# A two-layer graph network on one core: attention scores on four tiles of the array, and the softmax sums on two

## The chip, the core and the metric

The kernel runs on one core of a Trainium2 chip. The metric is the device time of one execution in microseconds (us), lower is better. All data is float32.

## The reference

`x` has 16 graphs of 1024 nodes with 256 channels. Layer 0 normalizes each node, builds a weighted adjacency from the difference of the nodes' channel means, makes queries from it, keys and values from the normalized nodes, and runs attention with four heads of 64 channels. Layer 1 normalizes again, multiplies by a normalized adjacency, and applies two linear maps with a batch norm each. Both layers add their result to `x`. The change lies in the attention of layer 0:

```python
q = jnp.transpose(g, (0, 2, 1)).reshape(B, N, h, hd).transpose(0, 2, 1, 3)
kv = (x @ kv_w).reshape(B, N, 2, h, hd).transpose(2, 0, 3, 1, 4)
k, v = (kv[0], kv[1])
scale = (1.0 + 1e-06) / (np.sqrt(hd) + 1e-06)
attn = jax.nn.softmax(jnp.einsum('bhnd,bhmd->bhnm', q, k) * scale, axis=-1)
out = jnp.einsum('bhnm,bhmd->bhnd', attn, v)
```

## The kernel before, in words

The 16 graphs go through `attention()` (L1032) in 64 **units**: a graph `b`, a pair of heads `k` (two heads of 64 channels fill the 128 partitions), and a half `f` of the 1024 queries (FB = 512). A unit has four **steps**; a step `g` takes two blocks `m` of 128 keys. So there are 256 steps. Each step issues on TensorE, in this order:

- `scores` (L906): for each of the two key blocks, one tile `sc` of two PSUM banks; for each head `e` of the pair a matmul (L914) whose weights are 64 channels by 128 keys and whose moving operand is 64 channels by 512 queries. Head 0 lies in rows 0 to 63 of the array, head 1 in rows 64 to 127. ScalarE then takes the exponential of the 128x1024 tile into `p` (L922).
- What `at_top` holds for this step: the `sums` (L977) of the unit before, or its `finish` (L1004), four transposes of 128x128.
- `values` (L946) of the step before: for each key block and head a matmul (L955) whose weights are 128 keys by 64 channels, so that head 0 fills array columns 0 to 63 and head 1 columns 64 to 127; they accumulate in `o` over the four steps of a unit.
- Pieces of the **background** (L818): everything else of the neighbouring graphs (queries, keys and values, layer 1's aggregation and first linear map). It is a chain of Python generators; each piece names a cost, and the loop at L1077 draws pieces until the cost done has reached the cost due at this step. Nearly all matmuls of the background go through `product` (L168), which splits a 128x128 weight block into two column halves of 64 (`HW`), each a matmul with all 128 rows.

The softmax isn't shifted by its maximum. The denominators come from VectorE: `add` (L935) sums the `p` tiles of a unit into `acc`; at the end of two steps `fold` (L966) transposes squares of `acc` and sums them into `part`. Three steps after the unit's last values, `sums` multiplies `part` (32 columns) by the constant matrix `same` in one matmul of 128x128 weights (L985), and three VectorE instructions (L993 to L1002) pick and invert the sums. One step later `finish` transposes the output and `add_output` scales it and adds it to `x`.

The order on every engine is the order of the Python calls (`manual_schedule`, L1421). Inside a step it is: scores, `at_top`, a piece of the background that asked for the top of a step (`TOP`, only in graph 0, two pieces with transposes), `adds`, `add`, `values`, background, `at_end`. For the last unit (`UNITS - 1`) sums and finish are one step after its last values, both in `at_top`.

After the loop comes `second` (L1143): the second linear map of layer 1 in matmuls of 128x128 weights (L1259), transposes back (L1390) and the output's DMAs. A second, shifted path (`shifted_attention`, L861) runs only if the sums leave a safe range; it isn't run here.

Of the kernel before, what the change touches and what calls it, by code (L numbers as in the profile page):

```python
# [17 lines left out]
P = 128  # L18
# [5 lines left out]
def gnn_two_layers_kernel(  # L24
# [12 lines left out]
    nc = tc.nc  # L37
# [6 lines left out]
    FB = 512  # L44
# [3 lines left out]
    HW = P // 2  # L48
# [27 lines left out]
    UNITS = B * CC * NH  # L76
# [20 lines left out]
    def layers(shifted):  # L97
# [23 lines left out]
        xs, hs, hts, ats, qs, ks, vs = {}, {}, {}, {}, {}, {}, {}  # L121
# [11 lines left out]
        def advance(pieces):  # L133

            due = queue[:]
            queue.clear()
            cost = next(pieces, None)
            for action in due:
                action()
            return cost  # L140

        def run(*parts):
            for part in parts:
                while advance(part) is not None:
                    pass
            while queue:
                queue.pop(0)()
# [20 lines left out]
        def product(dst, left, right, start, stop):  # L168

            for e in range(2):  # L170
                r = slice(e * HW, (e + 1) * HW)
                nc.tensor.matmul(dst[r], left[:, r], right, start=start, stop=stop)  # L172
# [645 lines left out]
        def background(b):  # L818

            if b == 0:  # L820
                differences(1)
                for k in range(CC):
                    yield TOP
                    transposed(1, k)
                    yield 1.0
                w, products, norm = weighers[1], keys_values(1), Norm(2, True).all()
                yield from weave(
                    islice(products, 4), (0, double(islice(w, 8))), (0, islice(norm, 4))
                )
                yield from weave(  # L830
                    plain_queries(1), (0, norm), (0, w), (5, graph()), (7, degrees())
                )
                differences(2)
                yield from islice(products, 2)
                yield from prepare(2, products)
                return
            before = hidden(b - 1)
            gather = aggregate(b - 1)
            if b + 1 < B:
                w, products, norm = weighers[b + 1], keys_values(b + 1), normed(b - 1)  # L840
                yield from weave(islice(products, 4), (0, islice(w, 4)))
                if b == 1:
                    load_later()
                yield from weave(queries(b + 1), (0, double(w)), (9, islice(norm, 5)))
                yield next(gather)
                yield from weave(products, (0, norm))
            else:
                yield from weave(endings.pop(), (2, normed(b - 1)))
                yield next(gather)
            if b + 2 < B:  # L850
                yield from weave(gather, (3, summed(b + 2)))
                yield from prepare(b + 2, before)
            elif b + 2 == B:

                yield from gather
                endings.append(before)
            else:
                yield from gather
                yield from weave(before, (0, normed_last()))
# [46 lines left out]
        def scores(b, k, f, g):  # L906


            made = []
            for m in (2 * g, 2 * g + 1):  # L910
                sc = ps_sc.tile([P, 2, FB], F32, tag="sc", name=f"sc_{b}_{k}_{f}_{m}")
                for e in range(2):
                    r = slice(e * HD, (e + 1) * HD)
                    nc.tensor.matmul(  # L914
                        sc[:, e, :],
                        ks[b][k][r, m * P : (m + 1) * P],
                        qs[b][k][r, f * FB : (f + 1) * FB],
                        start=True,
                        stop=True,
                    )  # L920
                pr = p4.tile([P, 2, FB], F32, tag="p", name=f"p_{b}_{k}_{f}_{m}")
                nc.scalar.activation(pr, sc, AF.Exp)  # L922
                made.append(pr)
            return made

        class Unit:
# [50 lines left out]
            def sums(self):  # L977

                b, k, f = self.at
                J = FB // P  # L980
                if k == f == 0:
                    invs[b] = p2.tile([P, CC, NH, J, 2], F32, tag="inv", name=f"inv_{b}")
                self.inv = invs[b][:, k, f]
                pt = ps_t.tile([P, FB], F32, tag="t", name=f"sums_{self.name}")[:, : 2 * J * NS]
                nc.tensor.matmul(  # L985
                    pt,
                    same.rearrange("p a r -> p (a r)"),
                    self.part.rearrange("p e c -> p (e c)"),
                    start=True,
                    stop=True,  # L990
                )
                tmp = p1.tile([P, 2 * J, NS + 1], F32, tag="group", name=f"group_{self.name}")
                nc.vector.tensor_mul(  # L993
                    tmp[:, :, :NS],
                    pt.rearrange("p (c a) -> p c a", a=NS),
                    group.unsqueeze(1).to_broadcast([P, 2 * J, NS]),
                )
                nc.vector.tensor_reduce(tmp[:, :, NS], tmp[:, :, :NS], AX.X, ALU.add)
                nc.vector.reciprocal(
                    self.inv.rearrange("p j e -> p e j"),  # L1000
                    tmp[:, :, NS].rearrange("p (e j) -> p e j", e=2),
                )  # L1002
# [29 lines left out]
        def attention():  # L1032

            units = [Unit(b, k, f) for b in range(B) for k in range(CC) for f in range(NH)]
            steps = [(u, g) for u in units for g in range(NG)]
            per_graph = CC * NH * NG
            before = None
            at_top, at_end, adds = {}, {}, {}
            bg, done, total, top = iter(()), 0.0, 0.0, False
            for s in range(len(steps) + 2):  # L1040
                if s < len(steps):
                    unit, g = steps[s]
                    b = unit.at[0]
                    if s % per_graph == 0:
                        run(bg)
                        top = False
                        bg, done = background(b), 0.0
                        total = (37.6 if b > 0 else 41.0) * (b + 1 < B) + 24.0 * (b > 0) + 4.0 * (b + 2 < B)
                        total += 13.7 * (0 < b < B - 2) + 27.4 * (b == B - 1) + 3.0 * (b == 0)

                        total -= 10.3 * (b == B - 1)
                    made = scores(*unit.at, g)
                    due = total * (s % per_graph + 1) / per_graph
                else:
                    due += 5.1
                for action in at_top.pop(s, ()):
                    action()
                if top:
                    done += advance(bg)
                    top = False  # L1060
                if s in adds:
                    adds.pop(s)()
                if s < len(steps):
                    for pr in made:
                        unit.add(pr)
                if before is not None:
                    (last, g_last), prs = before
                    last.values(g_last, prs)
                    if g_last == NG - 1:

                        one = (0, 0, 1, 1) if last.index == UNITS - 1 else (0, 1, 3, 4)
                        for e in range(2):
                            at_end.setdefault(s + one[e], []).append(lambda u=last, e=e: u.fold(e))
                        at_top.setdefault(s + one[2], []).append(last.sums)
                        at_top.setdefault(s + one[3], []).append(last.finish)
                        adds[s + one[3]] = last.add_output
                while done < due and not top:  # L1077
                    cost = advance(bg)
                    if cost is None:
                        break  # L1080
                    if cost == TOP:
                        top = True
                        break
                    done += cost
                for action in at_end.pop(s, ()):
                    action()
                before = (steps[s], made) if s < len(steps) else None
            run(bg)
# [375 lines left out]
```

## Time and profile before

| | |
|---|---|
| median of three runs | 2571.63 us (2571.38 to 2572.58) |
| the profiled execution's own time | 2572.44 us |
| its span, first to last instruction | 2570.6 us |
| granted TensorE clock, mean | 0.989 |
| score matmuls, records and busy | 2048, 510.7 us |
| values matmuls, records and busy | 2048, 495.9 us |
| sums matmuls, records and busy | 128, 26.3 us |
| attention loop, first to last score matmul | 62.3 to 2226.8 us |

In the profile PE is the matmuls on TensorE and PEld the weight loads, which run beside them. A group's line names the source line, engine, operation, output and inputs; then for matmuls the rows and columns of the array that one takes (64*128 is 64 rows by 128 columns), the shapes and the count. Starts are more reliable than ends: the ends of matmuls are modelled. `idle before` is the engine's idle time just ahead, with what released it.

### The profile page before, as it was taken

The numbers are of one execution on the slowest core, as the hardware profiler recorded it, in microseconds if no ns is written. First come the engines' busy times: TensorE is split into PE (matmuls) and PEld (weight loads), VectorE is DVE, ScalarE is ACT, GpSimd is POOL, SyncE is SP. The second block draws the span as 40 slices with busy tenths as digits, with TensorE's granted clock in tenths as the row PEclk, the third lists the DMA queues.
The fourth block names the chain that finished last, engine by engine and source line by source line (L and its number), as shares of the span: only waits on it lengthen the run. The fifth ranks groups of instructions, "written<-read, shape, count | busy, mean of one in ns | idle before, by whom it ended". The sixth has DMA issues, their size and how long they took to land. (4 is left out here: it accounts for less than half of the span.)

```text
span 2570.6 us, 31151 instructions
## 1 busy us (share of the span) xinstructions
PE 2497.0 (97%) x11403; PEld 913.0 (36%) x11403; DVE 1851.1 (72%) x2865; ACT 1432.0 (56%) x1978; POOL 396.8 (15%) x470
## 2 busy tenths in 40 slices
PE   8999999999999999999999999999999999999984
PEld 3333333333333333333333333333333333334443
DVE  4668786867777686878686777868686866656774
ACT  6765564647474746556464747464565634245553
POOL 1540100010101000010000010100101001036653
PEclk9999999999999999999999999999999999999997
DMA  4664425153434434351525344444425152255459
GB/s 140 211 223 146 157 85 198 58 205 99 173 128 155 148 148 135 110 181 61 209 70 185 119 158 142 156 136 151 139 95 194 45 187 96 103 217 213 174 199 364
DMA packets 149058, 392.81 MB, mean 153 GB/s; under 512 B 17304, under 2 KB 48544, under 8 KB 140960
## 3 DMA queue, kind: packets, MB, share of 16 engines
q1 hardware_dynamic: 126272, 297.39, 33.7%
q0 software_dynamic: 22624, 93.34, 9.5%
q8 instruction: 92, 1.51, 0.2%
q14 instruction: 70, 0.57, 0.1%
HBM read 301.47 MB, written 89.19 MB: 152 GB/s over the span
## 5 line engine op out<-in xcount | busy, mean ns | idle before, releaser
L922 ACT ACTIVATE p<-sc 128x1024 f32<-128x1024 f32 x512 | 495.1, 1020 | 495.5 <-PE sc L914 494.8
L944 DVE TENSOR_TENSOR acc<-acc,p 128x1024 f32<-128x1024 f32 x384 | 471.2, 1227 | 143.9 <-ACT p L922 123.2
L914 PE MATMUL sc<-q,k 64*128 64x512 f32 x2048 | 510.7, 617 | 6.5 <-ACT p L922 6.4
L955 PE MATMUL o<-p,v 128*64 128x512 f32 x2048 | 495.9, 605 | 0.0
L172 PE MATMUL pg<-w,h_a 128*64 128x512 f32 x1600 | 357.9, 592 | 3.0 <-DVE q L635 2.1
L172 PE MATMUL pa<-aht,h_b 128*64 128x512 f32 x1536 | 347.8, 595 | 3.5 <-ACT h_b L342 3.4
L914 PEld LDWEIGHTS sc<-q,k 64*128 64x128 f32 x2048 | 176.5, 186 | 328.9 <-issue 297.7
L481 ACT ACTIVATE w<-cbc,csum 128x512 f32<-128x512 f32 x256 | 285.5, 1167 | 0.0
L172 PE MATMUL py<-at,w 128*64 128x512 f32 x1024 | 230.7, 598 | 0.0
L468 DVE SCALAR_TENSOR_TENSOR w<-w,adj 128x1024 f32<-128x1024 f32 x128 | 157.4, 1230 | 87.5 <-ACT w L489 81.9
L955 PEld LDWEIGHTS o<-p,v 128*64 128x64 f32 x2048 | 124.1, 136 | 256.8 <-issue 243.3
L172 PEld LDWEIGHTS pg<-w,h_a 128*64 128x64 f32 x1600 | 114.6, 137 | 231.9 <-issue 213.4
L172 PEld LDWEIGHTS pa<-aht,h_b 128*64 128x64 f32 x1536 | 111.1, 137 | 217.5 <-issue 208.6
L769 POOL DMA_DIRECT2D y_d<-y x128 | 70.5, 551 | 701.9 <-ACT y L768 693.9
L768 ACT ACTIVATE y<-py,vec 128x512 f32<-128x512 f32 x128 | 87.5, 683 | 135.5 <-PE py L172 112.1
L94 POOL TENSOR_SCALAR lnsm_b<-mv_b 128x4 f32<-128x4 f32 x32 | 12.1, 379 | 834.5 <-DVE mv_b L320 834.4
L489 ACT ACTIVATE w<-w 128x1024 f32<-128x1024 f32 x128 | 135.2, 1056 | 1.7
L543 DVE TENSOR_TENSOR w<-w,w 128x1024 f32<-128x1024 f32 x112 | 132.7, 1215 | 1.5
L342 ACT ACTIVATE h_b<-x,lnsm_b 128x256 f32<-128x256 f32 x128 | 70.4, 608 | 110.4 <-DVE lnsm_b L331 110.4
L172 PEld LDWEIGHTS py<-at,w 128*64 128x64 f32 x1024 | 74.8, 138 | 147.2 <-issue 134.4
L172 PE MATMUL pk<-ht,kvw_f 128*64 128x512 f32 x512 | 117.9, 603 | 1.5 <-ACT ht L400 1.5
L172 PE MATMUL pv<-kvw_f,ht 128*64 128x256 f32 x1024 | 115.9, 379 | 0.0
(160 smaller groups left out, 2699.6 us busy)
## 6 DMA issues: line engine op xcount, KB each, us to landing
aht<-aht_d SPq DMA_DIRECT2D x224, 512.0 KB, 6.7
adj<-in_adj_dram SPq DMA_DIRECT2D x128, 512.0 KB, 5.6
y_d<-y POOLq DMA_DIRECT2D x128, 256.0 KB, 2.9
yin_f<-y_d SPq DMA_DIRECT2D x32, 1024.0 KB, 6.3
x<-in_x_dram SPq DMA_DIRECT2D x32, 512.0 KB, 5.2
para<-in_para_dram SPq DMA_DIRECT2D x64, 256.0 KB, 4.0
x_d<-x POOLq DMA_DIRECT2D x16, 1024.0 KB, 10.3
xo_f<-x_d SPq DMA_DIRECT2D x32, 512.0 KB, 8.8
```

The costliest lines, as they stand in the source:

```text
L172: nc.tensor.matmul(dst[r], left[:, r], right, start=start, stop=stop)
L342: nc.scalar.activation(self.h[:, t, :], self.src[:, t, :], AF.Relu, bias=self.sm[:, 1, t : t + 1], scale=self.sm[:, 0, t : t + 1], accum_o ...
L468: nc.vector.scalar_tensor_tensor(w, w, 1.0, a, op0=ALU.add, op1=ALU.mult)
L481: nc.scalar.activation(w[:, t, :].rearrange("p (t q) -> p t q", q=P), cbc[:, q * NT // NH : (q + 1) * NT // NH], AF.Abs, bias=csum[:, th * ...
L489: nc.scalar.activation(made[i], made[i], AF.Tanh, scale=-0.5 / C)
L543: nc.vector.tensor_sub(block(i)[part], block(x)[part], block(y)[part])
L768: nc.scalar.activation(y, made, AF.Identity, bias=b1[:, j : j + 1])
L769: nc.gpsimd.dma_start(out=y1_d[i][:, j, :], in_=y)
L914: nc.tensor.matmul(sc[:, e, :], ks[b][k][r, m * P : (m + 1) * P], qs[b][k][r, f * FB : (f + 1) * FB], start=True, stop=True,)
L922: nc.scalar.activation(pr, sc, AF.Exp)
L944: nc.vector.tensor_add(self.acc, self.acc, pr)
L955: nc.tensor.matmul(self.o[r, :], vs[b][k][:, m, r], pr[:, e, :], start=(m == 0), stop=(m == NT - 1),)
```

## The change

Each score matmul of 64 rows by 128 columns becomes two of 64 rows by 64 columns: 64 keys each, side by side in the array's columns, writing partitions 0 to 63 and 64 to 127 of the same bank. With the two heads in the two row halves, a key block takes four tiles of the array, in the order head 0 left, head 0 right, head 1 left, head 1 right. The sums' matmul goes through `product`, so it is two matmuls of 128 rows by 64 columns. A third table, `at_mid`, is added to the loop: it runs after a `TOP` piece of the background, where `at_top` runs before one; the sums of all units but the last are put there.

```diff
                 for e in range(2):
                     r = slice(e * HD, (e + 1) * HD)
-                    nc.tensor.matmul(
-                        sc[:, e, :],
-                        ks[b][k][r, m * P : (m + 1) * P],
-                        qs[b][k][r, f * FB : (f + 1) * FB],
-                        start=True,
-                        stop=True,
-                    )
+                    for c in range(2):
+                        part = slice(c * HW, (c + 1) * HW)
+                        nc.tensor.matmul(
+                            sc[part, e, :],
+                            ks[b][k][r, m * P + c * HW : m * P + (c + 1) * HW],
+                            qs[b][k][r, f * FB : (f + 1) * FB],
+                            start=True,
+                            stop=True,
+                        )
...
-                nc.tensor.matmul(
+                product(
                     pt,
                     same.rearrange("p a r -> p (a r)"),
                     self.part.rearrange("p e c -> p (e c)"),
-                    start=True,
-                    stop=True,
+                    True,
+                    True,
                 )
...
-            at_top, at_end, adds = {}, {}, {}
+            at_top, at_mid, at_end, adds = {}, {}, {}, {}
...
                 if top:
                     done += advance(bg)
                     top = False
+                for action in at_mid.pop(s, ()):
+                    action()
                 if s in adds:
                     adds.pop(s)()
...
-                        at_top.setdefault(s + one[2], []).append(last.sums)
+                        (at_top if last.index == UNITS - 1 else at_mid).setdefault(
+                            s + one[2], []
+                        ).append(last.sums)
                         at_top.setdefault(s + one[3], []).append(last.finish)
```

## The prediction

> **What bounds the kernel now.** I read the page's busy shares first, then the busy times by stretch, then the groups by shape, and last the order of time around one step of the attention loop.
>
> ```profile
> PE 2497.0 (97%) x11403; PEld 913.0 (36%) x11403; DVE 1851.1 (72%) x2865; ACT 1432.0 (56%) x1978; POOL 396.8 (15%) x470
> ```
> ```profile
> 200.00:2200.00 2000.00, 1997.26 (x9464) 701.23 (x9460) 1489.74 (x2303) 1125.64 (x1542) 161.36 (x252) 1.00 0.40 138
> ```
> The columns after the stretch and its length are the busy times of PE, PEld, DVE, ACT and POOL, then the granted clock. In the 2000 us that hold nearly all of the attention loop, TensorE is idle for 2.7 us; VectorE is busy for 74% and ScalarE for 56%. So each nanosecond that TensorE spends between its streams there is on the path, and the tail after 2290 us only shifts. But busy is not streaming; the groups and the order of time show the difference.
>
> ```profile
> L914 PE MATMUL sc<-q,k 64*128 64x512 f32 x2048 | 510.7, 617 | 6.5 <-ACT p L922 6.4
> L955 PE MATMUL o<-p,v 128*64 128x512 f32 x2048 | 495.9, 605 | 0.0
> L985 PE MATMUL sums<-part,same 128*128 128x32 f32 x128 | 26.3, 288 | 5.0 <-DVE part L973 5.0
> ```
> The third field is rows*columns of the array that one matmul takes. There are 256 steps with 4 score matmuls each in the code, and 2048 records: every fp32 matmul is two records (two passes), with a weight load each. Now one step, from the order of time; columns are start, length, engine, line, what, count:
>
> ```profile
> 1201.69 0.30 PEld L914 LDWEIGHTS sc<-q,k 64*128 64x128 f32 x4 [0.81 <-issue]
> 1201.69 1.99 PE L914 MATMUL sc<-q,k 64*128 64x512 f32 x8
> 1203.61 1.94 PE L955 MATMUL o<-p,v 128*64 128x512 f32 x8
> 1205.37 5.32 PE L172 MATMUL pg<-w,h_a 128*64 128x512 f32 x24
> 1210.62 1.99 PE L914 MATMUL sc<-q,k 64*128 64x512 f32 x8
> ```
> The starts are what counts. In the trace's single records two matmuls start 6 to 7 ns apart, on two tiles of the array, and the next two 0.423 us later: 0.43 us per pair. Twelve pairs of pg should take 5.155 us and take 1210.62 - 1205.37 = 5.25: **0.095 us lost** at the end, where the tile shape changes to 64*128. Four pairs of scores should take 1.72 us and take 1.92: 0.20 lost, of which the records place 0.105 before the second pair and 0.097 at the end. The values (1.72) take 1.76 to 1.77: 0.05 lost at their start, none at their end, because pg has their shape. The first score pair runs 693 ns against 589 for the others, the first values pair 643 against 592. So a change of shape costs a gap of 0.095 us, and then a weight load that nothing hides: 0.105 us for 128 columns, 0.052 for 64.
>
> Once per unit the sums stand between scores and values:
>
> ```profile
> 763.38 1.99 PE L914 MATMUL sc<-q,k 64*128 64x512 f32 x8
> 765.30 0.30 PEld L985 LDWEIGHTS sums<-part,same 128*128 128x128 f32 x2 [0.76 <-DVE w L543]
> 765.30 0.41 PE L985 MATMUL sums<-part,same 128*128 128x32 f32 x2
> 765.64 1.94 PE L955 MATMUL o<-p,v 128*64 128x512 f32 x8
> ```
> Without sums the values start 0.52 us after the last score record, with them 0.857 us: **0.338 us per unit**, for 32 columns of streaming. In the trace 63 of the 64 units have exactly this order.
>
> **What the Trainium skill says.** "TensorEngine Tiling (Array Packing)", Key Properties: changing the tiling mode drains TensorE, and tiles load and multiply independently. The trace agrees: 0.095 us at each change of shape, pairs on two tiles 7 ns apart. "TensorE: Matmul & The Clock Gate", LDWEIGHTS (loading the stationary operand): a load takes P/1.2 ns for P columns, whatever the rows; so 107 ns for 128 and 53 for 64, and the trace exposes 104 and 52. The same page, What overlaps and what doesn't, says matmuls keep strict program order; that doesn't fit the trace, where the second tile's first pass starts 7 ns after the first tile's, although the first tile's second pass stands ahead of it in the instruction stream. The same page's Measured speedup vs the span model gives 10.6 times for 16 tiles at once; no run here shows more than two tiles.
>
> **The change part by part**, against the profiled execution's own 2572.4 us (span 2570.6; the median of the three shown is 2571.6, 0.8 less, within what they scatter).
>
> *Scores in quarters.* Each score matmul becomes two of 64 rows by 64 columns, so 2048 records become 4096, and as many loads. Streaming: four tiles instead of two, each 512 columns twice, so one group of four per 0.43 us, as now one pair: **no change if four tiles run together.** For that I have the two halves separately: row halves run together in the scores, column halves in L172 and L955, each with its own load. Issue: a group is eight instructions per 0.43 us; L172's pv (256 columns) already has that, four matmuls (379 ns mean, a pair each 0.216 us) and four loads per 0.43 us, so I cost it at nothing, covered by the streaming. The instruction queue's own DMA is 0.2% of the engines' time, nothing too. Nothing else moves: no other engine's instruction, no DMA, no queue of SP or POOL.
>
> *Its switches.* The shape still changes on both sides (64*64 against 128*64: the rows differ). Does the gap stay? Scores to sums and scores to transposes (64*128 to 128*128, columns equal, rows different) start 0.519 us after the last score record, exactly as scores to values do, against 0.423 with no change. So a change of rows alone drains: gaps stay, 0. The exposed load becomes 64 columns wide: 0.052 instead of 0.105, 256 times: **-13.6 us**. Bounds: that, if loads of four tiles run together (loads of two rows' tiles and of two columns' tiles do, 7 ns apart), and 0, if the two row tiles of a column half load in turn. I take the first, since both directions are shown apart. Against it: two more starts 7 ns apart in front of each drain, 256 x 14 ns = **+3.6 us** (bounds 0 and 3.6: steady groups aren't lengthened, since a lone 128*128 matmul in L1259 has the same 0.43 spacing as a pair).
>
> *Sums in two column halves.* Now: load 107, load 107, stream 27 (32 of 512 columns), gap 95 = 336 ns; measured 338, so this account holds. After: shape 128*64 as the values. The first load of 52 lies where the values' first exposed load lay; added are 53 for the second pass and 53 for the values' load behind it, 27 ns of streaming hidden under each, and 7 ns of a second start: 114 ns. No gap follows. If loads and streams don't overlap, 167. So 338 - 114 = 224 ns, 63 times: **-14.1 us** (bounds -10.8 and -14.6). The move from at_top to at_mid changes nothing in 63 units: only a transposition due at the top of a step lies between, and both of those steps have no sums. The matmul waits for VectorE's part, written two steps earlier; queued behind the wait are the values, as now. VectorE's three instructions after it keep their place.
>
> Sum: -13.6 + 3.6 - 14.1 = **-24.1 us**: 2572.4 - 24.1 = 2548.3, less 0.8 for the median: **2547.5**. Bounds: -28.2 gives 2543.4, -7.2 gives 2564.4. Nothing is late next: ScalarE's exponentials have 44% of slack, and waits of TensorE in the loop are 6.4 us for the scores' own buffer.
>
> **Rivals.**
> *Slower: the four tiles don't run together.* The passes come in the order a, a', b, b', c, c', d, d'. To start b beside a, TensorE has to pass over one matmul and its load, which the trace shows; to start d it has to pass over three of each, which it doesn't show. If it sees only as far as the second tile, c and d start with a', the block takes one pass more: 256 x 0.43 = +110 us, 2657. If never more than two tiles run, the block takes four passes more: +440 us, 2988. It decides at the point where c's first pass starts later than some 20 ns after a's. For it: no shape 64*64 anywhere in the trace, and the skill's sentence on strict order. Against it: that order is already not kept, and the skill's 16 tiles.
> *Much faster: equal column halves need no drain.* Then the gap and the exposed load vanish on entering scores (256 x 0.152) and at the values where no transpose stands between (193 x 0.149): 68 us more, 2480. Against it: the rows-only changes above drain.
> *The narrow loads bring nothing*: the row tiles load in turn, only sums gain: -10.5, 2561. For it: unseen for four tiles. This lies in the range.
>
> **How the numbers follow.** Forecast 0.70, loads in turn 0.10, no drain 0.07, not together 0.13. The range, 2543 to 2565, is the bounds above rounded outward; it holds the forecast and the loads in turn, and leaves out the other two, 0.20. Within 0.2% (5 us) is about what a measurement of this kernel can't tell from no change: 0.01, the end of the loads-in-turn case. Faster 0.70 + 0.07 + 0.09 = 0.86, slower 0.13.
>
> **What would show it.** Right: a block of 16 score records still 1.86 to 1.88 us from start to start of the next, its first records some 641 ns against 589, four starts within some 21 ns; sums to values 0.11 to 0.17 us instead of 0.34; the gap of 0.095 still there. Wrong: score blocks of 2.3 us or more, or pairs 0.43 us apart inside them (not together); blocks near 1.72 (no drain).

## The result and the profile after

| | before | after |
|---|---|---|
| median | 2571.51 us (2570.99 to 2572.58) | 2552.94 us (2551.65 to 2554.47) |
| profiled execution, its span | 2572.44, 2570.6 us | 2551.71, 2549.8 us |

The ratio of after to before is 0.9928, 95% interval 0.991 to 0.9945: 18.6 us faster, where 24.1 were forecast. The spans of the two profiled executions differ by 20.8 us.

The page's busy shares and the stretch of the attention loop, after:

```profile
PE 2476.0 (97%) x13579; PEld 855.9 (34%) x13579; DVE 1849.1 (73%) x2865; ACT 1433.3 (56%) x1978; POOL 398.3 (16%) x470
```
```profile
200.00:2200.00 2000.00, 1995.05 (x11548) 654.41 (x11544) 1503.53 (x2322) 1131.31 (x1548) 161.69 (x252) 1.00 0.41 139
```
TensorE still sets the pace, with 2176 records more. But its idle time in this stretch has grown from 2.7 to 5.0 us: something new stops it. Now the two places that the prediction costed, in the order of time. A step without sums:

```profile
1191.68 0.21 PEld L916 LDWEIGHTS sc<-q,k 64*64 64x64 f32 x8 [0.81 <-issue]
1191.68 1.95 PE L916 MATMUL sc<-q,k 64*64 64x512 f32 x16
1193.56 1.94 PE L957 MATMUL o<-p,v 128*64 128x512 f32 x8
1195.33 5.32 PE L172 MATMUL pg<-w,h_a 128*64 128x512 f32 x24
1200.58 1.95 PE L916 MATMUL sc<-q,k 64*64 64x512 f32 x16
```
From start to start: 1.88 us for the scores (1.92 before), 1.77 for the values, and 5.25 for the 24 records of pg, the same as before. So the gap of 0.095 us at the change of shape is still there, and only the exposed load has become narrower. And a step with sums:

```profile
758.97 0.20 PEld L172 LDWEIGHTS sums<-part,same 128*64 128x64 f32 x4 [0.81 <-DVE w L543]
758.97 0.31 PE L172 MATMUL sums<-part,same 128*64 128x32 f32 x4
759.11 1.92 PE L957 MATMUL o<-p,v 128*64 128x512 f32 x8
```
The values start 0.14 us after the sums, where it was 0.34.

The groups name the new stop (the last field is the idle time just ahead and its releaser):

```profile
L916 PE MATMUL sc<-q,k 64*64 64x512 f32 x4096 | 500.4, 604 | 6.9 <-ACT p L924 6.9
L172 PE MATMUL pv<-kvw_f,ht 128*64 128x256 f32 x1024 | 118.8, 380 | 2.2 <-ACT v L672 2.2
```
The values' projection pv had no wait before; now it waits in 13 places for ScalarE's copies. From the single records, adding up the times from each matmul's start to the next, by pair of groups, gives the whole account of the 20.8 us: scores to scores -10.3; sums (to the values, to each other, and the values' first interval behind them) -9.7 - 2.9 - 1.3 = -13.9; **pv to pv +5.1**; py and pk, background products that nobody touched, -2.0; the rest +0.3.

The 2.0 us of py and pk come from the clock that TensorE was granted at their place. In the stretches below, before and then after, the same 24 records of py (12 pairs) run; in the second line of each the third figure from the end is the mean granted clock.

```profile
2245.21 7.89 PE L172 MATMUL py<-at,w 128*64 128x512 f32 x24
2245.20:2253.10 7.90, 7.90 (x27) 2.46 (x28) 4.63 (x12) 3.28 (x6) 1.08 (x2) 0.68 0.09 33
```
```profile
2225.70 6.71 PE L172 MATMUL py<-at,w 128*64 128x512 f32 x24
2225.70:2232.40 6.70, 6.70 (x27) 2.23 (x28) 4.63 (x12) 3.28 (x6) 1.08 (x2) 0.80 0.10 39
```
The trace's clock record has TensorE at 0.5 from 2243.5 to 2250.3 us before, and from 2221.6 to 2228.4 after. While it is at 0.5, the pairs of py start 0.82 to 0.90 us apart instead of 0.423: six pairs before, three after. The slow pairs of pk lie ahead of the first clock record (18.0 us before, 16.6 after) and have the same spacing: six before, four after (the last of each somewhat faster). No trace was kept of the other executions, so it isn't shown why the medians are 18.6 us apart and not 20.8.

### The profile page after: what moved, and what is told of

It is laid out like the page before. It is cut to its first block, busy times and chain, and to the rows that moved or that the text cites. A ratio compares the mean times of both kernels' runs of the same rounds, so it can differ in the third digit from the quotient of the medians.

```text
span 2549.8 us, 35503 instructions
## 1 busy us (share of the span) xinstructions
PE 2476.0 (97%) x13579; PEld 855.9 (34%) x13579; DVE 1849.1 (73%) x2865; ACT 1433.3 (56%) x1978; POOL 398.3 (16%) x470
## 4 chain that ended last, share of the span: by engine, by line
PE 69%; DVE 17%; ACT 8%; issue 2%; DMA 2%; POOL 0%; SPq 0%; POOLq 0%; DVEq 0%; ACTq 0%
PE pa L172 15%; PE sc L916 14%; PE o L957 13%; PE py L172 9%; PE m_f L1265 7%; PE pk L172 4%; DVE acc L946 4%; DVE w L543 4%; ACT w L481 3%; PE pv L172 2%; PE pg L172 2%; ACT p L924 2%; DMA out_dram<-xo_f 2%; DVE st_b L318 1%; DVE w L468 1%
## 5 line engine op out<-in xcount | busy, mean ns | idle before, releaser
L916 PE MATMUL sc<-q,k 64*64 64x512 f32 x4096 | 500.4, 604 | 6.9 <-ACT p L924 6.9
L916 PEld LDWEIGHTS sc<-q,k 64*64 64x64 f32 x4096 | 131.5, 132 | 350.1 <-issue 318.6
L342 ACT ACTIVATE h_b<-x,lnsm_b 128x256 f32<-128x256 f32 x128 | 70.5, 610 | 115.7 <-DVE lnsm_b L331 115.7
```

The costliest lines, as they stand in the source:

```text
L916: nc.tensor.matmul(sc[part, e, :], ks[b][k][r, m * P + c * HW : m * P + (c + 1) * HW], qs[b][k][r, f * FB : (f + 1) * FB], start=True, sto ...
```

## The experiments

The questions: do both parts bring what they were costed at, what is the wait at pv, and how far does the result of the scores hang on four tiles running together?

**Each part alone.** e1_scores is the kernel before with this edit only:

```diff
-                        sc[:, e, :],
-                        ks[b][k][r, m * P : (m + 1) * P],
...
+                            sc[part, e, :],
+                            ks[b][k][r, m * P + c * HW : m * P + (c + 1) * HW],
```


> The kernel before with the scores in quarters alone; sums as one matmul of 128x128 weights. Theory (a narrower exposed load, four starts instead of two ahead of the drain, gaps unchanged): score blocks shrink from 1.92 to 1.88 us, 256 times: -10 us against before, so about 2561.5 us, and at most 2 us of it given back in the wait of the values product for its bank. Rival (rows-only changes cost less than I read, or the quarters are faster in themselves): more than -14 us. Rival (the quarters gain nothing and all came from the sums): 2571.

Measured: 2563.34 us against 2571.57 of before on the same chip, ratio 0.9967 (0.9955 to 0.9979): -8.2. In its trace scores to scores takes 9.9 us less, and pv to pv 2.1 more. Both are close to the theory's -10 and its at most 2.

e2_sums is the kernel before with the sums through `product` and in `at_mid`:

```diff
-                nc.tensor.matmul(
+                product(
                     pt,
```


> The kernel before with the sums in two column halves just ahead of the values, scores as before (64*128). Theory: sums to values shrink from 0.857 to 0.66 us with the values' first load hidden, 63 times 0.215 us: -13.5 us, so about 2558 us if nothing is given back; if the wait of the values product for ScalarE's copies (seen in the changed kernel, 13 times 0.39 us) is caused by TensorE coming early after a step with sums, then 5 us of it are given back here too: 2563. If that wait needs both parts, or comes from the shorter score blocks, then 2558.

Measured: 2559.21 us, ratio 0.9952 (0.9938 to 0.9965): -12.4. The sums' intervals fall by 9.7 + 3.0 + 1.3 = 14.0 us, as in the full change within 0.1, and pv takes 2.5 us more. So neither part alone makes the whole wait: pv's late product starts on average 0.323 us after the one before in e1_scores, 0.349 in e2_sums, 0.547 in the changed kernel, and 0.209 before. It is the later the more TensorE has gained in the steps ahead, whichever part gained it. My sharper alternatives for e2_sums (all 5 us or none) both fell; the wait grows with the gain.

The move to `at_mid` was not run by itself. In the traces of before and e2_sums, which has it, the groups of matmuls follow one another in the same order on TensorE, so it moved nothing there.

**The wait at pv.** The order of time around one late product, in the changed kernel:

```profile
1202.81 0.74 DVE L318 BATCH_NORM_STATS2 st_b<-x 128x6 f32<-128x256 f32 x2
1203.47 0.30 DVE L320 BATCH_NORM_AGGREGATE mv_b<-st_b 128x2 f32<-128x6 f32 x2
1203.68 1.26 DVE L529 TENSOR_TENSOR q<-q,para 128x512 f32<-128x512 f32 x2
1204.22 3.62 PE L172 MATMUL pv<-kvw_f,ht 128*64 128x256 f32 x32
1204.37 1.23 ACT L531 ACTIVATE q<-q 128x512 f32<-128x512 f32 x2 [0.36 <-DVE q L529]
1205.51 1.92 ACT L924 ACTIVATE p<-sc 128x1024 f32<-128x1024 f32 x2
1207.32 0.65 ACT L672 COPY v<-pv 128x256 f32<-128x256 f32 x2
1208.02 1.95 PE L172 MATMUL pv<-kvw_f,ht 128*64 128x256 f32 x16 [0.17 <-ACT v L672]
```
Read from the bottom: the third pv product needs one of two PSUM banks. It is freed by the copies at L672, which end at 1207.97; the product was due at 1204.22 + 2 x 1.73 = 1207.68. ScalarE does them after two exponentials, those after the queries' relu (L531), and the relu waits for VectorE's multiplications (L529), which stand behind statistics of layer 1's norm (L318 and L320). Seen from the start of the step's scores (1200.58), L529 starts after 3.10 us. In the kernel before, where that step starts at 1210.62, the same lines are

```profile
1213.33 1.26 DVE L529 TENSOR_TENSOR q<-q,para 128x512 f32<-128x512 f32 x2
1214.31 5.35 PE L172 MATMUL pv<-kvw_f,ht 128*64 128x256 f32 x48
1216.96 0.65 ACT L672 COPY v<-pv 128x256 f32<-128x256 f32 x2
```
There L529 starts after 2.71 us, the copies end at 1217.61, and the third product was due at 1214.31 + 2 x 1.73 = 1217.77: it was covered by 0.16 us. The other graphs are alike: in all 13 the copies end 0.14 to 0.16 us before the product is due in the kernel before, and 0.28 to 0.30 us after that in the changed one. VectorE has hardly a break in this stretch (in the changed kernel none over 0.11 us from 1171 to 1205 us), so it didn't become faster with TensorE; against TensorE it came 0.39 us later, and the cover was gone. e3_norm3 takes VectorE's work away from there; `norm` yields layer 1's norm in pieces, of which three instead of five are now woven into the queries:

```diff
-                yield from weave(queries(b + 1), (0, double(w)), (9, islice(norm, 5)))
+                yield from weave(queries(b + 1), (0, double(w)), (9, islice(norm, 3)))
```


> The changed kernel, with two pieces of layer 1's norm (VectorE's statistics of four tiles and ScalarE's first two relus) taken from behind the queries and put beside the values product: three pieces woven into the queries instead of five. Theory (the third values product of 13 graphs waits for a PSUM bank, because ScalarE's copies stand behind exponentials that stand behind the queries' relu, which waits for VectorE): VectorE reaches the queries' multiplications about 1 us earlier, the wait is gone, and the time falls by some 5 us, to about 2547 to 2549. Rival (the wait comes from ScalarE's or TensorE's own order, not from VectorE's queue): the wait of 0.55 us stays in 13 places and the time stays at 2552 to 2554; or the relus beside the values product make new waits and it gets longer.

> The changed kernel once more, beside the others on the same chip: 2552 to 2554 us, and 13 values products with a start 0.54 to 0.56 us after the one before instead of 0.21.

Measured on the same chip: e3_norm3 2546.74 us, ratio to before 0.9902 (0.9887 to 0.9918); the changed kernel again 2553.12, ratio 0.993 (0.9916 to 0.9943). The late products are gone (pv's group has its old numbers), and the repeat of the changed kernel has its 13 again:

```profile
L172 PE MATMUL pv<-kvw_f,ht 128*64 128x256 f32 x1024 | 115.9, 379 | 0.0
```
The order of time of e3_norm3 at that place, where the scores start at 1198.61:

```profile
1200.84 1.29 DVE L529 TENSOR_TENSOR q<-q,para 128x512 f32<-128x512 f32 x2
1201.55 1.23 ACT L531 ACTIVATE q<-q 128x512 f32<-128x512 f32 x2 [8.74 <-DVE q L529]
1202.25 4.92 PE L172 MATMUL pv<-kvw_f,ht 128*64 128x256 f32 x44
1204.50 0.65 ACT L672 COPY v<-pv 128x256 f32<-128x256 f32 x2
```
L529 comes after 2.23 us instead of 3.10, the copies after 5.89 instead of 6.74, and in the 13 graphs they end 0.56 to 0.58 us before the product is due. The shift also takes two relus of ScalarE (L342) away from ahead of L531; but in the changed kernel ScalarE stood idle for 0.36 us between them and L531, until VectorE's L529 (the line at 1204.37), so VectorE set the time there. The span is 2544.2 us, 26.4 below before: more than the 24.1 that the prediction summed. It could be that this shift saves time whatever else is changed, so e7_before_norm3 makes it in the kernel before, alone:

> The kernel before (no part of the change) with the same shift of the norm's pieces as in e3_norm3: three woven into the queries, not five. Theory (the shift only removes the wait that the change opened): nothing to remove here, so within 2.5 us of before, 2569 to 2573, and no values product late. Rival (the shift saves time by itself, and the change has nothing to do with it): 5 to 6 us faster here too, 2566.

Measured: 2572.3 against 2572.34 us, ratio 0.9999 (0.9991 to 1.0008). The shift brings nothing without the change. Of its 6.4 us, 5.1 are the wait at pv, which the change had opened. Another 1.6 us of its trace are the clock again: the changed kernel has TensorE at 0.5 from 2143.1 to 2146.5 us, with pairs of pa 0.84 us apart, the kernel before from 2161.6 to 2165.0, and e3_norm3 has no such stretch there. One trace doesn't show whether the shift removed it. The 26.4 us hold these 1.6 and the 2.0 of py and pk, so they are no gain of the two parts beyond what was forecast. e3_norm3 is also the fastest kernel of this study.

**How far tiles run together.** The slower rival rested on the order of the passes. Two kernels stretch it. e4_keys32 splits the scores into eight tiles of 64 rows by 32 columns (`NS` is 4, `SQ` 32):

```diff
-                    for c in range(2):
-                        part = slice(c * HW, (c + 1) * HW)
+                    for c in range(NS):
+                        part = slice(c * SQ, (c + 1) * SQ)
...
-                            ks[b][k][r, m * P + c * HW : m * P + (c + 1) * HW],
+                            ks[b][k][r, m * P + c * SQ : m * P + (c + 1) * SQ],
```


> The changed kernel with the scores in quarters of 32 keys: eight tiles of 64 rows by 32 columns at once, 32 instructions per 0.86 us on TensorE instead of 16. Theory (tiles run together as far as the array is split, and issue is covered by streaming): exposed load 26 instead of 52 ns (-6.7 us), eight starts 7 ns apart instead of four ahead of each drain (+7 us): within 3 us of the changed kernel, score blocks of 1.88 us. Rival (each instruction of TensorE costs some 50 ns of issue, which the changed kernel just hides): a group of eight matmuls and eight loads takes 0.8 us instead of 0.43, and the whole gets 380 us longer. Rival (TensorE passes over a limited number of waiting matmuls; the eighth tile stands behind seven of them): the group is skewed, one pass more per block, 110 us longer.

Measured (one run): 2552.28 us, and in the order of time

```profile
449.35 0.18 PEld L916 LDWEIGHTS sc<-q,k 64*32 64x32 f32 x16 [0.81 <-issue]
449.35 1.95 PE L916 MATMUL sc<-q,k 64*32 64x512 f32 x32
451.23 0.31 PE L172 MATMUL sums<-part,same 128*64 128x32 f32 x4
```
The block is 1.88 us from start to start with 32 matmuls and 32 loads in it, as with 16 and 16. The first eight matmuls run 613 ns, so 24 ns of load are exposed instead of 51, and their starts spread over 47 ns instead of 20. The two cancel, and neither issue nor passing over shows up.

e5_back puts four passes of one tile in a row, both key blocks, ahead of the next tile:

```diff
-            for m in (2 * g, 2 * g + 1):
-                sc = ps_sc.tile([P, 2, FB], F32, tag="sc", name=f"sc_{b}_{k}_{f}_{m}")
-                for e in range(2):
...
+            for e in range(2):
+                r = slice(e * HD, (e + 1) * HD)
+                for c in range(2):
+                    part = slice(c * HW, (c + 1) * HW)
+                    for m, sc in zip(ms, scs):
```


> The changed kernel with the 16 passes of a step's scores in another order: for each of the four tiles first both key blocks, four passes of one tile in a row, then the next tile. The fourth tile's first pass stands behind 12 matmuls and 12 loads instead of 6 and 6. Theory (each tile has its own queue, deep enough): the four tiles still start within some 21 ns, the block stays at 1.88 us; ScalarE gets the first key block 0.43 to 0.86 us later, which costs little, since its exponentials are not on the path: within 10 us of the changed kernel. Rival (TensorE passes over only a few waiting matmuls): the later tiles start 0.43 us or more after the first, blocks of 2.3 us or more, 110 us longer or more.

Measured (one run): 2562.62 us, 10 longer than the changed kernel, at the edge of what was expected. The four tiles still start together, though the last stands behind 12 matmuls and 12 loads:

```profile
467.02 0.23 PEld L919 LDWEIGHTS sc<-q,k 64*64 64x64 f32 x8 [0.81 <-issue]
467.03 1.97 PE L919 MATMUL sc<-q,k 64*64 64x512 f32 x16
468.92 0.65 PE L961 MATMUL o<-p,v 128*64 128x512 f32 x2
```
But their starts are 13 ns apart and not 7, so they spread over 40 ns and not 21 as I expected. From first to last start a block takes 1.378 us at the median against 1.358 in the changed kernel: 256 x 0.02 = 5 us. Another 6 us lie in 17 blocks. Twelve of them, one per graph, are each 0.156 us longer; the first is

```profile
316.48 1.94 ACT L928 ACTIVATE p<-sc 128x1024 f32<-128x1024 f32 x2 [0.32 <-PE sc L919]
318.31 2.12 PE L919 MATMUL sc<-q,k 64*64 64x512 f32 x16
```
Here only the first tile starts at 318.31; the other three start 0.17 to 0.20 us later, just after ScalarE's two exponentials have ended at 318.42. In the order of the calls they stand behind the first tile's second key block, and that writes the tile `sc` which the second exponential was still reading. So it had to wait, and what stood behind it waited too. The other five blocks are 0.8 to 0.9 us longer each; one of them lies in a stretch at half clock, the other four I have not followed.

## Why the prediction was right, and where it was not

- **Four tiles run together: right.** Four starts within 20 ns, steady groups of four 0.43 us apart, no change in streaming. This was the point at which the slower rival would have decided. e4_keys32 shows the same for eight tiles and e5_back for 12 matmuls passed over, so nothing speaks for that rival.
- **Gaps stay, the load is halved: right.** The first matmuls run 640 ns against 589, so 51 ns of load are exposed. The terms -13.6 and +3.6 make -10.0; the trace of e1_scores has -9.9, that of the changed kernel -10.3. The rivals "no drain" and "loads in turn" are both refuted by the blocks of 1.88 us.
- **Sums: right.** -14.1 forecast, -13.9 measured. What the sums still cost, two loads and one more start, was taken as 114 ns; the records give 117. Together the two parts brought 24.2 us in the trace, as forecast.
- **"Nothing is late next": wrong.** This is the step that failed, and it is the 5 us by which the gain fell short. I argued from averages: ScalarE at 56%, and TensorE's waits in the loop. Cover is local: in 13 graphs one product was covered by 0.14 to 0.16 us. Before it TensorE gained about 0.45 us on ScalarE's copies (0.40 against the start of the step, 0.04 by its shorter score block), so they ended some 0.29 us after the product was due; it started 0.05 later, and 0.05 of a load was no longer hidden: 13 x 0.39 = 5.0. e3_norm3 and e7_before_norm3 show that this wait, and not a mis-sized part, is the difference.
- The 2.0 us that py and pk lost are luck as far as the forecast goes: fewer of their pairs fell into a stretch at half clock, which stood in no term of the sum. py lost 0.8 to 1.5 us in every trace with a part of the change and 0.1 in that of e7_before_norm3, so its share may go with the change; no run shows what sets where such a stretch begins.

In the skill's terms: the drain at a change of tiling mode and the load's cost by columns, as "TensorEngine Tiling (Array Packing)", Key Properties, and "TensorE: Matmul & The Clock Gate", LDWEIGHTS (loading the stationary operand), state them, carried the forecast, and the runs agree: a gap of 0.095 us at each change of shape, and 24, 51 and 104 ns of load exposed for 32, 64 and 128 columns.

## What to carry to other kernels

Where TensorE changes the shape of its tiles, look at starts, not at busy time: here a change cost a gap of about 0.1 us and one exposed load that goes with the columns, so it paid to make the tiles narrower at the change (down to 64 columns; at 32 the greater number of starts took back what the load saved), and to give a small product the shape of its neighbour. When a bounding engine is made faster, ask at each of its waits how much cover it has in that place, in tenths of a microsecond; average shares of the other engines don't answer that. Before a remainder of a microsecond or two is put down to a change, look at the granted clock where it lies. A few pieces of work moved away from such a place can win back what a good change gives up.

## What the runs showed of the hardware that I had not expected

- Matmuls of different tiles don't keep program order: a tile's first pass started beside the others though up to 12 matmuls and 12 loads stood ahead of it. The starts of four tiles with four instructions each (two loads, two matmuls) are 6.7 ns apart, those of tiles with eight instructions each 13 ns: by these two figures, an estimate of 1.7 ns for each instruction passed over. An instruction that waits for its buffer is not passed over: in 12 blocks of e5_back it held back the three tiles behind it for 0.17 to 0.20 us.
- 32 matmuls and 32 loads ran in a block of 1.88 us, 29 ns for an instruction; the block was no longer than with half as many, so no limit of issue showed.
